# Gate logits computed with the gate's weights stationary on four column quarters, then turned by one transpose

## The chip, the cores and the metric

The kernel runs on one core of one Trainium2 chip. The core has a matrix engine (TensorE, "PE" in the profile, with its weight loads listed apart as "PEld"), a vector engine (VectorE, "DVE"), an engine for activation functions (ScalarE, "ACT"), a general engine (GpSimd, "POOL") and a queue engine that issues most transfers (SyncE, "SP"). Data lies in SBUF, 128 partitions wide; matrix products land in PSUM. The metric is the device time of one execution in microseconds (us). The kernel before took 2319.12 us (median of 3 runs, 2315.53 to 2322.49).

## What is computed

The input x has 16 sequences of 512 tokens with 256 features, all float32. One transformer layer is applied:

```python
x = x + attention(layernorm(x))          # 16 heads of 64, tanh soft clamp at 50, causal
t = layernorm(x)                         # 8192 tokens
shared = gelu(t @ sw1 + sb1) @ sw2 + sb2
probs = softmax(t @ gate_w + gate_b)     # gate_w is 256 x 8: one logit per expert
topk_p, topk_i = top_k(probs, 2)
combine = zeros(T, 8) with topk_p at topk_i
h = gelu(einsum('td,edf->etf', t, w1) + b1)
y = einsum('etf,efd->etd', h, w2) + b2
x = x + einsum('te,etd->td', combine, y) + shared
```

The change concerns `t @ gate_w` alone: for one sequence, 512 tokens by 256 features times 256 features by 8 experts.

## The kernel before, in words

The main loop runs over 16 sequences and, within each, over 8 pairs of heads (steps p = 0 to 7). A step does the score products of the next pair (`s`, line 272), attends for the present one (`av` and `sums`, lines 323 and 332), and projects queries and keys of the pair after next (`pq`, line 249). ACT clamps and exponentiates the scores (lines 287 and 288). VectorE divides by the row sums (`oT`: two reciprocals on line 342 and a product on line 343).

The rest of the layer is spread over the steps of the following sequence by the function `around`. Call the sequence whose attention is finished `done`. At p = 0 and 1 its output projection is made, at p = 1 its second layernorm; at p = 3 its normalised rows are turned (`x2T`, the tile of 128 features by 2 by 512 tokens), and after the two `pq` products of that step come the hidden layer of the shared expert (`hidden`, tile `ph`, line 695, then Gelu on ACT, line 703) and the gate (`gate`, tile `pg`, line 367). At p = 4 `place` ranks the tokens' choices within the group (`pos`, lines 414 and 415; `slot`, line 417), `transposed_comb` turns the table of shares (`pc`, line 685), two value projections follow (`pv`, line 232), and `expert_out` finishes the shared expert (`py`, lines 714 and 722).

The gate goes on after its product, all on VectorE but one activation: add the bias (`lg`, line 375), subtract the maximum (lines 377, 378), Exp on ACT (`pr`, line 380), normalise (lines 382 to 384), compare all pairs of experts to get each expert's rank (lines 389 to 394), and set the shares (`comb`, line 398).

Fifteen sequences are routed: their rows are scattered to DRAM by expert, and later read back in tiles of 256 rows for the routed experts (`rh`, `pr` of line 573, `ry`, on lines 586, 573 and 604). This work is a list of "fillers", of which `around` runs a few at the end of each step once a group of sequences (9, then 6) is complete. The last sequence is not routed but computed densely.

The order on PE is as written (the block runs under a manual schedule for PE); the other engines' orders are fixed by a scheduler when the program is built. Every engine executes its own list in order. PSUM tiles come from pools of two buffers: `ps_m` (tag "m": `pq`, `pg`, `pos`, `pc`, `pv`, `py` and others) and `ps_s` (tag "s": `s`, `ph`, the turned rows, `rh`). In this order the tile `ph` has the same bank as the second score tile `s` of the next step, so that this score product waits until Gelu has read `ph`.

A float32 product is two matrix instructions, each with its own weight load; a transpose is one. So the 8 products of one gate are 16 instructions in the profile. In those of line 367 the tokens are stationary (a 128 by 128 piece of `x2T`) and the gate's weights, 8 columns, stream past.

Of the kernel before, what the change touches and what calls it, by code (L numbers as in the profile page):

```python
# [9 lines left out]
F32 = mybir.dt.float32  # L10
# [5 lines left out]
P = 128  # L16
# [8 lines left out]
def preln_attention_moe_kernel(  # L25
# [15 lines left out]
    nc = tc.nc  # L41
# [4 lines left out]
    NT = N // P  # L46
    KD = D // P
    E = gate_w.shape[2]
# [4 lines left out]
    const = ctx.enter_context(tc.tile_pool(name="const", bufs=1))  # L53
    xp = ctx.enter_context(tc.tile_pool(name="xp", bufs=3))
    work = ctx.enter_context(tc.tile_pool(name="work", bufs=2))
    small = ctx.enter_context(tc.tile_pool(name="small", bufs=2))
# [3 lines left out]
    ps_m = ctx.enter_context(tc.tile_pool(name="ps_m", bufs=2, space=bass.MemoryType.PSUM))  # L60
# [11 lines left out]
    def sync_dma(to, of):  # L72
        with queued():
            last["dma"] = nc.sync.dma_start(to, of).ins
        return last["dma"]
# [32 lines left out]
    def weights(name, ap, queue):  # L108
        t = const.tile(list(ap.shape), F32, tag=name, name=name)
        queue.dma_start(t, ap)  # L110
        return t
# [3 lines left out]
    wq_sb = weights("wq_sb", wq, nc.sync)  # L115
    wk_sb = weights("wk_sb", wk, nc.scalar)
    wo_sb = weights("wo_sb", wo, nc.sync)
    gw_sb = weights("gw_sb", gate_w, nc.sync)
    gb_sb = const.tile([P, E], F32, tag="gb_sb", name="gb_sb")
    nc.sync.dma_start(gb_sb, gate_b.to_broadcast([P, E]))  # L120
    b1_sb = weights("b1_sb", b1, nc.sync)
# [4 lines left out]
    ident = const.tile([P, P], F32, tag="ident", name="ident")  # L126
# [59 lines left out]
    def layernorm(src, name):  # L186

        mv = small.tile([P, NT, 2], F32, tag="mv", name=f"mv_{name}")
        for t in range(NT):
            st = small.tile([P, 6], F32, tag="st", name=f"st_{name}_{t}")  # L190
            nc.vector.bn_stats(st, src[:, t, :])
            nc.vector.bn_aggr(mv[:, t, :], st)
        ve = small.tile([P, NT], F32, tag="ve", name=f"ve_{name}")
        nc.vector.tensor_scalar(ve, mv[:, :, 1], EPS, None, ALU.add)
        rstd = small.tile([P, NT], F32, tag="rstd", name=f"rstd_{name}")
        nc.gpsimd.tensor_tensor(rstd, ve, neg_half, ALU.pow)
        xn = work.tile([P, NT, D], F32, tag="xn", name=f"xn_{name}")
        for t in range(NT):
            nc.vector.tensor_scalar(  # L199
                xn[:, t, :],  # L200
                src[:, t, :],
                mv[:, t, 0:1],
                rstd[:, t : t + 1],
                ALU.subtract,
                ALU.mult,
            )
        return xn
# [138 lines left out]
    def project_out(b, h):  # L346

        xt = x_tiles[b]
        po = ps_m.tile([P, 2, D], F32, tag="m", name=f"po_{b}_{h}")
        for u in range(2):  # L350
            t = 2 * h + u
            for c in range(NP):
                nc.tensor.matmul(  # L353
                    po[:, u, :],
                    oTs[b, c][:, t * P : (t + 1) * P],
                    wo_sb[:, c, :],
                    start=(c == 0),
                    stop=(c == NP - 1),
                )
        nc.vector.tensor_add(xt[:, 2 * h : 2 * h + 2, :], xt[:, 2 * h : 2 * h + 2, :], po)  # L360

    def gate(b, xT):

        pg = ps_m.tile([P, NT, E], F32, tag="m", name=f"pg_{b}")
        for t in range(NT):
            for k in range(KD):
                nc.tensor.matmul(
                    pg[:, t, :],
                    xT[:, k, t * P : (t + 1) * P],
                    gw_sb[:, k, :],  # L370
                    start=(k == 0),
                    stop=(k == KD - 1),
                )
        lg = small.tile([P, NT, E], F32, tag="lg", name=f"lg_{b}")
        nc.vector.tensor_add(lg, pg, gb_sb.unsqueeze(1).to_broadcast([P, NT, E]))
        mx = small.tile([P, NT], F32, tag="mx", name=f"mx_{b}")
        nc.vector.tensor_reduce(mx, lg, AX.X, ALU.max)
        nc.vector.tensor_sub(lg, lg, mx.unsqueeze(2).to_broadcast([P, NT, E]))
        pr = small.tile([P, NT, E], F32, tag="pr", name=f"pr_{b}")
        nc.scalar.activation(pr, lg, AF.Exp)  # L380
        sm = small.tile([P, NT], F32, tag="sm", name=f"sm_{b}")
        nc.vector.tensor_reduce(sm, pr, AX.X, ALU.add)
        nc.vector.reciprocal(sm, sm)
        nc.vector.tensor_mul(pr, pr, sm.unsqueeze(2).to_broadcast([P, NT, E]))
        other = pr.unsqueeze(2).to_broadcast([P, NT, E, E])
        own = pr.unsqueeze(3).to_broadcast([P, NT, E, E])
        eq = small.tile([P, NT, E, E], F32, tag="table", name=f"eq_{b}", bufs=2)
        gt = small.tile([P, NT, E, E], F32, tag="table", name=f"gt_{b}", bufs=2)
        nc.vector.tensor_tensor(eq, other, own, ALU.is_equal)
        nc.vector.tensor_tensor(gt, other, own, ALU.is_gt)  # L390
        nc.vector.tensor_mul(eq, eq, before.unsqueeze(1).to_broadcast([P, NT, E, E]))
        nc.vector.tensor_add(gt, gt, eq)
        rank = small.tile([P, NT, E], F32, tag="rank", name=f"rank_{b}")
        nc.vector.tensor_reduce(rank, gt, AX.X, ALU.add)
        comb = small.tile([P, NT, 32], F32, tag="comb", name=f"comb_{b}")
        nc.gpsimd.memset(comb, 0.0)
        nc.gpsimd.memset(comb[:, :, E : E + 1], 1.0)
        nc.vector.scalar_tensor_tensor(
            comb[:, :, :E], rank, 1.5, pr, ALU.is_lt, ALU.mult
        )  # L400
        return comb, rank, pr
# [288 lines left out]
    def hidden(b, e, xT, w):  # L690
        ph = ps_s.tile([P, FC, N], F32, tag="s", name=f"ph_{b}_{e}")
        hT = work.tile([P, FC, N], F32, tag="hT", name=f"hT_{b}_{e}", bufs=2)
        for f in range(FC):
            for k in range(KD):
                nc.tensor.matmul(  # L695
                    ph[:, f, :],
                    w[:, k, f * P : (f + 1) * P],
                    xT[:, k, :],
                    start=(k == 0),
                    stop=(k == KD - 1),  # L700
                )
        for f in range(FC):
            nc.scalar.activation(hT[:, f, :], ph[:, f, :], AF.Gelu, bias=b1_sb[:, e, f : f + 1])
        return hT
# [49 lines left out]
        for _ in range(min(n, len(fillers))):  # L754
            fillers.popleft()()

    xTs, xns, gated, hTs = {}, {}, {}, {}
    units = range(len(UNITS))

    def early(b, p):  # L760
# [7 lines left out]
    def around(b, p, fill):  # L768

        done, more = b - 1, b + 1 < B  # L770
        group = group_of.get(done)
        if p == 0 and done >= 0:
            project_out(done, 0)
        if p == 1 and done >= 0:
            project_out(done, 1)
            xns[done, 1] = layernorm(x_tiles[done], f"f{done}")
        if p == 2:
            if more:
                xns[b + 1, 0] = layernorm(x_tiles[b + 1], f"a{b + 1}")
            if b < B:  # L780
                project_v(b, 2, xTs[b])
        if p == 3 and done >= 0:
            hTs[done] = hidden(done, SH, xTs[done, 1], sw1_sb)
            gated[done] = gate(done, xTs[done, 1])
        if p == 4:
            if done >= 0:
                comb, rank, pr = gated[done]
                if group:
                    place(done, rank, pr)
                gated[done] = comb, transposed_comb(done, comb)  # L790
            if b < B:
                project_v(b, 3, xTs[b])
        if p == 5 and more:
            project_v(b + 1, 0, xTs[b + 1])
        if p == 6 and more:
            project_v(b + 1, 1, xTs[b + 1])
        fill(p)
        if p == 4 and done >= 0:
            expert_out(done, SH, hTs.pop(done), sw2_sb, *gated[done])
            if group:  # L800
                scatter(done, xns.pop((done, 1)))
                sync_dma(
                    group.kept[done - group.first].rearrange("(t p) d -> p t d", p=P),
                    x_tiles.pop(done),
                )
                if done == group.first + group.count - 1:
                    tabulate(group)
                    fillers.extend(routed_steps(group))
                    fillers.append(lambda: pack(group))
                    fillers.extend(gather_steps(group))  # L810
                    pace["left"], pace["due"] = (B - 1 - b) * sum(WEIGHT), 0.0
                    if b == B - 1:
                        pace["left"] = 5 * len(fillers) // 6
        if p == 4 and b + 2 < B:
            load_x(b + 2)

    with tc.manual_schedule(engines={mybir.EngineType.PE}):
# [8 lines left out]
        for s in range(B * NP):  # L826
            b, p = divmod(s, NP)
# [12 lines left out]
        b = B - 1  # L840
# [68 lines left out]
```

## Time and profile before

| | |
|---|---|
| median of 3 runs | 2319.12 us |
| the profiled execution | 2317.56 us, of which the span of instructions is 2315.8 us |
| PE busy | 2209.4 us (95% of the span), 10968 matrix instructions |
| VectorE, ACT, POOL busy | 1102.8, 1037.9, 952.3 us |
| gate products, line 367 | 256 instructions, 29.6 us busy, 251 ns mean |
| hidden layer of the shared expert, line 695, one sequence | 8 instructions in 3.4 us |
| one sequence without fillers | 117.5 us (the gate starts at 190.65 and next at 308.19 us) |

Busy times count each instruction from its start to its modelled end, and matrix instructions overlap, so a difference of starts says more about what an instruction costs its queue. The chain of waits follows the work back from the last instruction to what released it; its durations add up to the span.

### The profile page before, as it was taken

How to read it: one execution, taken by the hardware profiler on the slowest of the kernel's cores; microseconds unless marked ns; L12 is line 12 of the kernel's file. 1: busy time of each engine (PE TensorE's matmuls, PEld its weight loads, DVE VectorE, ACT ScalarE, POOL GpSimd, SP SyncE). 2: the span in 40 equal slices, each digit the busy share in tenths (PEclk: the TensorE clock that was granted, in tenths of full speed). 3: DMA queues.
4: the chain of work that ended last, by engine and by line, in shares of the span. 5: the costliest groups of instructions: out<-in, count | busy, mean ns of one | idle time of the engine just before them, and what ended most of it. 6: DMA issues, size and time to landing. Idle time of an engine off the chain costs nothing.

```text
span 2315.8 us, 29554 instructions
## 1 busy us (share of the span) xinstructions
PE 2209.4 (95%) x10968; PEld 1405.6 (61%) x10968; DVE 1102.8 (48%) x1858; ACT 1037.9 (45%) x1352; POOL 952.3 (41%) x1091
## 2 busy tenths in 40 slices
PE   7999999999999999999999999999999799899996
PEld 3555555556565555555667677667655465558874
DVE  3445454545363636363644434444446555453334
ACT  3544444444444545444444554554554444351211
POOL 3444443435353535344423412422455847450025
PEclk9999999999999999999999999999999999999999
DMA  5001010101010101010142342342230503035776
GB/s 191 1 1 37 1 37 1 37 1 37 1 37 1 37 1 37 1 37 1 37 147 59 118 128 64 101 128 82 84 97 20 153 7 119 21 100 168 224 228 208
DMA packets 119855, 161.34 MB, mean 70 GB/s; under 512 B 12320, under 2 KB 90144, under 8 KB 119200
## 3 DMA queue, kind: packets, MB, share of 16 engines
q1 hardware_dynamic: 107760, 125.62, 17.5%
q0 software_dynamic: 11520, 31.47, 4.4%
q10 hardware_dynamic: 432, 2.36, 0.3%
q8 instruction: 87, 1.43, 0.3%
q14 instruction: 56, 0.46, 0.1%
HBM read 99.64 MB, written 59.77 MB: 69 GB/s over the span
## 4 chain that ended last, share of the span: by engine, by line
PE 76%; DVE 11%; DMA 5%; issue 3%; ACT 3%; POOL 2%; SPq 0%; POOLq 0%; DVEq 0%; ACTq 0%
PE pq L249 15%; PE s L272 10%; PE av L323 10%; PE po L353 9%; PE pv L232 8%; PE ry L604 5%; PE rh L586 5%; DVE oT L342 4%; PE sums L332 4%; DMA part<-ys,packed 3%; PE ph L695 2%; PE py L714 2%; DVE xn_a L199 2%; PE pr L573 1%; PE py L722 1%
## 5 line engine op out<-in xcount | busy, mean ns | idle before, releaser
L287 ACT ACTIVATE pe<-s 128x768 f32<-128x768 f32 (+1 forms) x384 | 334.5, 874 | 704.8 <-PE s L272 679.1
L342 DVE RECIPROCAL oT<-sums 128x256 f32<-128x256 f32 x256 | 430.9, 1724 | 355.3 <-PE sums L332 355.2
L291 POOL TENSOR_SCALAR_AFFINE_SELECT pe<-pe 128x256 f32<-128x256 f32 (+1 forms) x384 | 192.0, 501 | 902.0 <-ACT pe L288 847.4
L272 PE MATMUL s<-qk 64*128 64x512 f32 (+3 forms) x2048 | 345.4, 456 | 11.9 <-ACT qk L256 11.5
L288 ACT ACTIVATE pe<-pe 128x768 f32<-128x768 f32 (+1 forms) x384 | 349.5, 914 | 10.9
L323 PE MATMUL av<-pe,v 128*64 128x512 f32 (+3 forms) x2048 | 307.8, 443 | 34.5 <-DVE oT L343 34.4
L272 PEld LDWEIGHTS s<-qk 64*128 64x128 f32 x2048 | 176.6, 186 | 200.7 <-issue 144.9
L323 PEld LDWEIGHTS av<-pe,v 128*64 128x64 f32 x2048 | 140.3, 138 | 241.7 <-issue 208.7
L249 PE MATMUL pq<-xT_a,wq_sb 128*128 128x512 f32 x512 | 252.8, 617 | 0.8 <-DVE xT_a L217 0.8
L249 PE MATMUL pq<-xT_a,wk_sb 128*128 128x512 f32 x512 | 241.6, 595 | 5.0 <-DVE x L360 3.5
L232 PE MATMUL pv<-wv_sb,xT_a 128*128 128x256 f32 x1024 | 233.6, 382 | 4.4 <-DVE xT_a L217 4.4
L303 POOL TENSOR_TENSOR added<-pe,pe 128x768 f32<-128x768 f32 x128 | 232.3, 1814 | 10.5
L256 ACT COPY qk<-pq 128x512 f32<-128x512 f32 x256 | 149.8, 585 | 178.0 <-PE pq L249 178.0
L232 PEld LDWEIGHTS pv<-wv_sb,xT_a 128*128 128x128 f32 x1024 | 195.1, 192 | 52.0 <-issue 24.4
L353 PE MATMUL po<-wo_sb,oT 128*128 128x256 f32 x1024 | 226.3, 380 | 0.0
L353 PEld LDWEIGHTS po<-wo_sb,oT 128*128 128x128 f32 x1024 | 195.2, 191 | 38.7 <-issue 14.3
L653 POOL DMA_INDIRECT part<-ys,packed x120 | 117.2, 977 | 154.4 <-DMA dw<-in_w 99.6
L249 PEld LDWEIGHTS pq<-xT_a,wk_sb 128*128 128x128 f32 x512 | 97.7, 191 | 129.1 <-issue 120.4
L595 ACT ACTIVATE rhT<-rh,biases 128x256 f32<-128x256 f32 x148 | 62.0, 470 | 253.5 <-PE rh L586 253.4
L307 POOL TENSOR_TENSOR added<-added,pe 128x512 f32<-128x512 f32 x128 | 163.5, 1277 | 10.7
L239 DVE COPY v<-pv 128x512 f32<-128x512 f32 x128 | 87.3, 689 | 144.9 <-PE pv L232 144.9
L586 PE MATMUL rh<-rT,ew 128*128 128x256 f32 x592 | 142.6, 385 | 6.3 <-DVE rT L577 5.5
(134 smaller groups left out, 2302.4 us busy)
## 6 DMA issues: line engine op xcount, KB each, us to landing
ew<-in_w SPq DMA_DIRECT2D x148, 256.0 KB, 3.1
rows<-xs SPq DMA_DIRECT2D x74, 256.0 KB, 3.1
ys<-y SPq DMA_DIRECT2D x74, 256.0 KB, 3.3
x<-in_x SPq DMA_DIRECT2D x16, 512.0 KB, 4.0
xs<-zeros SPq DMA_DIRECT2D x32, 256.0 KB, 4.3
kept<-x SPq DMA_DIRECT2D x15, 512.0 KB, 3.0
acc<-kept SPq DMA_DIRECT2D x60, 128.0 KB, 2.9
out<-acc SPq DMA_DIRECT2D x60, 128.0 KB, 2.4
```

The costliest lines, as they stand in the source:

```text
L232: nc.tensor.matmul(pv[:, u], xT[:, k, t * P : (t + 1) * P], wv_pairs[:, k, :, 2 * g : 2 * g + 2, :], start=(k == 0), stop=(k == KD - 1),)
L249: nc.tensor.matmul(pq, w[:, k, p * P : (p + 1) * P], xT[:, k, :], start=(k == 0), stop=(k == KD - 1),)
L272: nc.tensor.matmul(ps[:, i, at : at + w], qk[rows, 1, j * P : (j + 1) * P], qk[rows, 0, j * P :], start=True, stop=True,)
L287: nc.scalar.activation(pe[:, :, :w], ps[:, :, :w], AF.Tanh, scale=CLAMP_IN)
L288: nc.scalar.activation(pe[:, :, :w], pe[:, :, :w], AF.Exp, scale=SOFTCLAMP)
L291: nc.gpsimd.affine_select(out=diagonal, in_=diagonal, compare_op=ALU.is_ge, fill=0.0, base=0, pattern=[[0, 2], [0, n], [1, P]], channel_mu ...
L303: nc.gpsimd.tensor_tensor(added, pair_pe[b, p, 0][:, :, P:], pe[:, :, : N - P], ALU.add)
L307: nc.gpsimd.tensor_tensor(added[:, :, P:], added[:, :, P:], pe[:, :, : 2 * P], ALU.add)
L323: nc.tensor.matmul(po[i * DH : (i + 1) * DH, j * P :], v[:, j, i, p % 2, :], pair_pe[b, p, u][:, i, at : at + w], start=(j == 0), stop=(j ...
L342: nc.vector.reciprocal(oT[:, half], sums[:, half])
L353: nc.tensor.matmul(po[:, u, :], oTs[b, c][:, t * P : (t + 1) * P], wo_sb[:, c, :], start=(c == 0), stop=(c == NP - 1),)
L586: nc.tensor.matmul(ph[:, f, :], tile["w1"][:, d, f * P : (f + 1) * P], tile["T"][:, d, :], start=(d == 0), stop=(d == KD - 1),)
```

## The change

The gate's weights become the stationary operand. They are padded with zeros from 8 to 32 columns, and the four token tiles of 128 tokens go to four column quarters of the PE array, each of which holds the same padded weights: the product of tile t writes partitions 32t to 32t + 31 of one PSUM tile `pl` (128 by 128: expert down, token across). There are still 8 products, 16 instructions. VectorE copies `pl` to SBUF (`logits`), and one transpose on PE brings tokens back to the partitions (`pg`, now 128 by 128, of which 4 by 8 columns are used).

The function is cut in two. `gate` (products and copy) is called before `hidden`, and `choose` (the transpose and all that came after the product) behind it. On PE the order was `pq`, `ph`, `pg`; it is now `pq`, `pl`, `ph`, `pg`. On VectorE the copy stands between the product of line 343 and `lg`; ACT's list is the same. At the start POOL clears the padded weights with its first fill of the kernel's own, and the load of `gate_w` on SP's queue, fourth there, writes 2 by 8 of the 2 by 32 columns.

```diff
-    gw_sb = weights("gw_sb", gate_w, nc.sync)
+    gw_sb = const.tile([P, KD, 32], F32, tag="gw_sb", name="gw_sb")
+    nc.gpsimd.memset(gw_sb, 0.0)
+    nc.sync.dma_start(gw_sb[:, :, :E], gate_w)
...
+    gated = {}
+
     def gate(b, xT):
-        pg = ps_m.tile([P, NT, E], F32, tag="m", name=f"pg_{b}")
-        for t in range(NT):
-            for k in range(KD):
+        pl = ps_m.tile([P, P], F32, tag="m", name=f"pl_{b}")
+        for k in range(KD):
+            for t in range(NT):
                 nc.tensor.matmul(
-                    pg[:, t, :],
+                    pl[t * 32 : (t + 1) * 32, :],
+                    gw_sb[:, k, :],
                     xT[:, k, t * P : (t + 1) * P],
-                    gw_sb[:, k, :],
                     start=(k == 0),
                     stop=(k == KD - 1),
                 )
+        logits = small.tile([P, P], F32, tag="combT", name=f"logits_{b}")
+        nc.vector.tensor_copy(logits, pl)
+        gated[b] = logits
+
+    def choose(b):
+        pt = ps_m.tile([P, P], F32, tag="m", name=f"pg_{b}")
+        nc.tensor.transpose(pt, gated[b], ident)
+        pg = pt.rearrange("p (t e) -> p t e", e=32)[:, :, :E]
         lg = small.tile([P, NT, E], F32, tag="lg", name=f"lg_{b}")
         nc.vector.tensor_add(lg, pg, gb_sb.unsqueeze(1).to_broadcast([P, NT, E]))
...
         if p == 3 and done >= 0:
+            gate(done, xTs[done, 1])
             hTs[done] = hidden(done, SH, xTs[done, 1], sw1_sb)
-            gated[done] = gate(done, xTs[done, 1])
+            gated[done] = choose(done)
```

## The prediction

> **What bounds the kernel now.** I read the page first. PE is busy for 95% of the span, which suggests that every matrix instruction saved is time saved. Part 4 of the page says otherwise in part:
>
> ```profile
> PE 2209.4 (95%) x10968; PEld 1405.6 (61%) x10968; DVE 1102.8 (48%) x1858; ACT 1037.9 (45%) x1352; POOL 952.3 (41%) x1091
> ...
> PE 76%; DVE 11%; DMA 5%; issue 3%; ACT 3%; POOL 2%; SPq 0%; POOLq 0%; DVEq 0%; ACTq 0%
> ```
>
> PE is 76% of the chain that ended last; 11% is VectorE, 3% ACT. So there are places where PE, though busy, is ahead of what decides. I then asked the chain of waits in order of time for one sequence around its gate (start, length, what):
>
> ```profile
> 181.20 0.86 PE sums L332 x8
> 182.06 0.85 PE s L272 x8
> ...
> 183.94 3.44 PE pq L249 x8
> 187.37 3.45 PE ph L695 x8
> ...
> 190.85 1.26 ACT hT L703 x2
> ...
> 193.42 0.24 ACT pr L380
> ...
> 202.29 0.16 DVE slot L417
> 202.45 0.04 issue
> 202.50 0.33 PE pc L685
> ...
> 213.16 2.31 PE av L323 x16
> ...
> 230.82 3.63 PE pq L249 x8
> ```
>
> The reader is to see what is missing. After `ph` the chain leaves PE: Gelu on ACT, a table load (192.13 to 193.41), Exp for `pr`, then twenty VectorE instructions up to `slot`, and it comes back to PE at `pc`. `pg` isn't in it. In the timeline `lg` and its two followers end at 193.17, and Exp starts at 193.42, just after the table load: the gate's product is 0.24 us early. From 193.68 to `slot` VectorE has no gap over 0.04 us (its two long reciprocals, 3.28 us, stand in that queue behind the ranking). PE does its work meanwhile and then waits, which the groups by line confirm:
>
> ```profile
> L367 PE MATMUL pg<-gw_sb,x2T_f 128*128 128x8 f32 x256 | 29.6, 251 | 0.0
> L685 PE MATMUL pc<-ident,comb 128*128 128x128 f32 x16 | 5.2, 325 | 4.5 <-DVE slot L417 4.5
> ```
>
> `pc` waits for `slot` 0.28 us in nearly every sequence. So between the end of `ph` and `pc` the path runs over ACT and VectorE, and PE has nothing to give there. Where fillers follow the gate it is different; the chain there, for the tenth gate:
>
> ```profile
> 1288.07 3.43 PE ph L695 x8
> 1291.51 1.69 PE pg L367 x16
> 1293.19 1.83 PE rh L586 x8
> ```
>
> Here `pg` is on the chain. By the timeline, of the 16 gates 12 are followed at once by scores `s` (the first nine and numbers 13 to 15), and 4 by fillers (10 to 12, and the last).
>
> **The change, part by part.**
>
> *What leaves `pg`'s place.* 16 instructions at a pitch of 0.111 us: 1.70 us before `rh`, 1.78 before `s` (differences of starts). One transpose comes there instead: `pr` of line 573 takes 0.44 us for 4 in the chain, so 0.11 us.
>
> *What is put before `ph`.* I call the delay of `ph` d. It has three terms.
>
> 1. Streaming. Instructions on column halves overlap: `sums` streams 4 x 128 + 4 x 384 = 2048 columns in 0.86 us, 0.42 ns a column, and `pq` on the full array 4096 in 3.44, 0.84 ns. Two halves go in the time of one. No row shows four quarters. The new products stream 16 x 128 = 2048 columns: 0.43 us if four overlap, 0.86 if two, 1.72 if none. I take four, since two halves lost nothing, and keep the others as ends. For four instructions starting one after another I add 0.03.
>
> 2. Going into another division of the array. `av` comes after row halves: 5120 columns at 0.42 ns are 2.15 us, the chain shows 2.31, so 0.16. I take that; a quarter's weight load is shorter, so 0.10 is the low end, the 0.20 of the next term the high one.
>
> 3. Going back to the full array. `pq` takes 3.63 us after row halves (230.82) and 3.44 after transposes on the full array (183.94): 0.19 to 0.20. `s` after column halves agrees: 4 x 256 + 4 x 128 columns at 0.42 are 0.65, the row shows 0.85.
>
> So d = 0.43 + 0.03 + 0.16 + 0.20 = 0.82 us, from 0.73 to 1.3, or 2.1 without overlap. Before, PE went from `pq` to `ph` in one division and paid neither 2 nor 3; the switch on the way to `s` is paid with and without the change.
>
> The Trainium skill (TensorEngine Tiling, Key Properties) says that a change of tiling mode drains the array. The rows of terms 2 and 3 agree, at 0.16 to 0.20 us. The page (When to Use Tiling) also recommends just this swap for an operand of at most 32 columns, with up to four times the speed; by that alone the 1.70 us would fall to an estimate of 0.43, plus 0.11 for the transpose, and 16 gates would save 19 us. The drain, and the place, speak against that.
>
> *Twelve gates followed by scores.* `ph` ends d later; Gelu, table load, `pr`, the VectorE queue, `slot` and `pc` all follow d later, since each starts when the one ahead ends. The product's 0.24 us of earliness grows, which buys nothing. PE gains 1.78 - 0.11 - 0.82 = 0.85 us and loses it again twice: the second score tile waits until Gelu has read `ph` in the same bank (Gelu ended at 192.11, the tile started at 193.38; now Gelu ends at 192.93 and PE would be there at 192.53, so 0.4 us of new wait), and at `pc` PE waits the rest, some 1.2 us in place of 0.28. Behind `pc` PE goes on without a gap. Each costs +0.82: 12 x 0.82 = +9.8 us.
>
> *Four gates followed by fillers.* PE is the path: 0.82 + 0.11 - 1.69 = -0.76 each, -3.0 us. ACT would hold them if its Gelu for `rh` came too late: it moves from 1296.50 to 1297.32, and PE asks for that bank at about 1297.32. That is even, so at most 0.1 us is lost. In the tail the chain goes by transfers that start from these products, so its 0.76 may get lost too: between -3.0 and -2.2.
>
> *The rest, at nothing.* The copy of `pl` (0.28 us by the 128x128 copy of line 687) is one more VectorE instruction between 186.6 and 192.5, where that engine is idle for 5.9 us; the transpose needs it only after 3.4 us of `ph`. Without that cover it would cost 0.28 + 0.1 per gate. `pl` needs what `ph` needed (`x2T`, ready 186.77, asked at 187.2) and the bank of the first `pq` tile (copied by 186.28). At the start one POOL fill (0.15 us) precedes the identity, which is done at 1.6 us and needed at 14.28; SP's load of `gate_w` is issued at 2.31, long after that fill; behind it in SP's queue are biases and zero fills, and the next x, whose transfer is issued at 26.5 us and read at 33.5. Its extra descriptors lie between nothing and the 0.74 us that this issue takes now. One `v` copy stands behind a fourth normalisation there (0.35 us); its reader comes later than 43 us.
>
> *Sum.* +9.8 - 3.0 = +6.8 us on the profiled execution's own time: 2317.56 + 6.8 = 2324.4. That execution is 1.56 us under the median of the three, so I predict 2325.9, +0.29%. A measurement here tells about 0.3%, 7 us, from no change; the forecast stands just at that bound.
>
> **The rivals.**
>
> *A. PE decides everywhere (faster).* Then each gate is worth -0.76 to -0.85 and 16 give -13 us: 2306. For it speaks the 95%. Against it, `pg` is not in the chain of 12 gates and `pc` waits for `slot`. It would need `slot` to come over 0.85 us before PE; it comes 0.28 after.
>
> *B. Quarters overlap less (slower, more).* Two at a time: d = 1.25, 12 x 1.25 - 4 x 0.33 = +13.7, 2332.8. None: d = 2.11, +27.4, 2346.5. For it: no row shows four. Against: halves overlap without loss.
>
> *C. The delay is absorbed.* The same sequence has a wait of 1.3 us of `av` for `oT` at p = 3. If its releaser didn't move with PE, the 9.8 us would vanish and -3.0 remain: 2316. Against: that chain starts from a score product of PE itself, and runs over ACT, POOL and the layernorm back to PE, so it moves too.
>
> *D. Switching is cheap between full and quarters:* d = 0.46, 12 x 0.46 - 4 x 1.12 = +1.0, 2320. Against: three kinds of switch in the rows cost 0.16 to 0.20.
>
> **How the numbers follow.** Forecast, with d from 0.73 to 0.95 (+4.9 to +8.8 us with the tail's doubt, 2324 to 2328): 0.62, of which 0.33 over the bound and 0.29 under it. A: 0.05. B: 0.19 (two at a time 0.15, none 0.04). C and D: 0.14. Slower by over 0.3%: 0.33 + 0.19 = 0.52; within: 0.29 + 0.14 = 0.43; faster: 0.05. The range reaches down to D, 2320, and up to two at a time, 2333; it leaves out A, none, and C's lower half, some 0.15.
>
> **What would show it.** Line 367's successor: 16 instructions per gate on 32 columns in about 0.43 us, `ph` starting 0.6 to 0.7 us after `pq`'s stream ends and its second product 0.1 later still. `lg` far earlier than the end of the table load. The second score tile waiting for Gelu, 0.4 us, 12 times; `pc` waiting 1.2 us; `pl` in the chain ahead of `ph`. Distance of gates without fillers: 117.5 + 0.8 = 118.4 us. The forecast is wrong if that distance falls, which means A, or if `pl` spreads over 0.9 us, which means B.

## The result and the profile after

The changed kernel takes 2328.15 us (median of 6, 2325.55 to 2329.58) beside 2318.97 us before: ratio 1.004, 95% interval 1.0026 to 1.0054. A second set, taken later, gave 2326.97 beside 2319.08 us: 1.0035, 1.0023 to 1.0047. So the change makes the kernel slower by 8 to 9 us; predicted were 2325.9 us and a range of 2320 to 2333. The profiled execution took 2325.55 us (span 2323.8), 8.0 us more than that of before.

First the page of the changed kernel, part 1 and the chain by engine:

```profile
PE 2204.0 (95%) x10984; PEld 1378.7 (59%) x10984; DVE 1101.4 (47%) x1874; ACT 1036.3 (45%) x1352; POOL 950.1 (41%) x1092
...
PE 74%; DVE 12%; issue 5%; DMA 3%; ACT 3%; POOL 3%; SPq 0%; DVEq 0%; another core or an unknown queue 0%; POOLq 0%; ACTq 0%
```

PE has less to do than before (2204.0 against 2209.4 us) and a smaller part in the chain (74% against 76%): it waits more. The groups of the gate's products, its transpose, and the product that waits for the ranking (count and form, then busy us and mean ns, then idle time ahead):

```profile
L371 PE MATMUL pl<-x2T_f,gw_sb 128*32 128x128 f32 x256 | 10.3, 279 | 0.0
L698 PE MATMUL pc<-ident,comb 128*128 128x128 f32 x16 | 5.2, 325 | 9.3 <-DVE slot L430 9.3
L385 PE MATMUL pg<-ident,logits 128*128 128x128 f32 x16 | 4.4, 272 | 0.0
```

The gate's products fell from 29.6 to 10.3 us busy. The wait at `pc` doubled, from 4.5 to 9.3 us in all. The chain of waits around the first gate (start, length, what) says what stands ahead of that wait:

```profile
184.22 3.44 PE pq L251 x8
187.66 0.57 PE pl L371 x16
188.24 3.64 PE ph L708 x8
...
191.90 1.19 ACT hT L716 x2
...
193.18 1.28 ACT L393
...
198.50 3.28 DVE oT L344 x2
201.78 0.56 DVE ahead L424
...
203.35 0.10 DVE slot L430
...
203.50 0.33 PE pc L698
```

`pl` is now a link of the chain, between `pq` and `ph`. From Gelu (`hT`) to `slot` the chain takes 203.35 - 191.90 = 11.45 us; before it took 202.29 - 190.85 = 11.44. The path over ACT and VectorE kept its length and starts later.

PE's timeline for the same gate shows what PE gained and where it gave it back (start, time to the last end, instruction, tile, count; idle time ahead and its releaser in brackets). Before:

```profile
185.49 1.88 PE L249 MATMUL pq<-xT_a,wk_sb 128*128 128x512 f32 x4
...
192.42 1.77 PE L272 MATMUL s<-qk 64*128 64x512 f32 x8
...
201.69 0.30 PE L414 MATMUL pos<-chosen,earlier 128*128 128x32 f32 x2
...
202.50 0.33 PE L685 MATMUL pc<-ident,comb 128*128 128x128 f32 x1 [0.28 <-DVE slot L417]
```

and after the change:

```profile
185.78 1.88 PE L251 MATMUL pq<-xT_a,wk_sb 128*128 128x512 f32 x4
187.59 0.65 PE L371 MATMUL pl<-x2T_f,gw_sb 128*32 128x128 f32 x16
188.16 3.70 PE L708 MATMUL ph<-x2T_f,sw_sb 128*128 128x512 f32 x8
191.70 0.27 PE L385 MATMUL pg<-ident,logits 128*128 128x128 f32 x1
191.90 1.13 PE L274 MATMUL s<-qk 64*128 64x512 f32 x4
193.22 0.92 PE L274 MATMUL s<-qk 64*128 64x384 f32 x4 [0.19 <-ACT hT L716]
...
201.62 0.30 PE L427 MATMUL pos<-chosen,earlier 128*128 128x32 f32 x2
202.39 0.41 PE L428 MATMUL pos<-ahead,ones 128*128 128x32 f32 x2 [0.46 <-DVE ahead L424]
203.50 0.33 PE L698 MATMUL pc<-ident,comb 128*128 128x128 f32 x1 [0.69 <-DVE slot L430]
```

I read such a timeline by differences of starts, since ends are modelled. From the start of the last `pq` tile to the first `s`: 6.93 us before, 6.12 after, a gain of 0.81. From there to `pos`: 9.27 and 9.72, so 0.45 lost while the second score tile waits for Gelu. From `pos` to `pc`: 0.81 and 1.88, so 1.07 lost while PE waits for VectorE. Together +0.71 us. The first eight such gates all show it (I call the 12 that scores follow direct gates, the others filler gates): their distance is 117.54 or 117.55 us before and 118.26 or 118.27 after.

The rest of the run, by starts of `ph` of the k-th gate in the traces, with three traces of each kernel (the second and third are among the runs below) and what the prediction's steps give for each stretch:

| stretch | before, three traces | after, three traces | forecast |
|---|---|---|---|
| start to 1st | 187.21, 187.74, 188.00 | 188.16, 188.56, 188.50 | +0.82 |
| 1st to 9th | 940.33, 940.38, 940.38 | 946.11, 946.13, 946.09 | +6.56 |
| 9th to 10th | 160.36, 160.37, 160.37 | 158.90, 159.22, 158.98 | +0.82 |
| 10th to 12th | 340.01, 340.01, 340.01 | 338.71, 338.72, 338.71 | -1.52 |
| 12th to 13th | 145.94, 148.53, 148.78 | 146.69, 146.72, 146.85 | -0.76 |
| 13th to 14th | 131.15, 131.72, 131.49 | 135.73, 131.34, 135.51 | +0.82 |
| 14th to 16th | 280.30, 279.85, 281.27 | 278.91, 279.36, 278.72 | +1.64 |
| 16th to the end | 130.50, 129.41, 129.79 | 130.63, 126.99, 132.88 | -1.58 |
| span | 2315.81, 2318.01, 2320.08 | 2323.84, 2317.04, 2326.25 | +6.8 |

The upper half is steady to some tenths; the lower half, where rows are gathered and scattered, moves by several us from one execution to the next, in both kernels.

### The profile page after: what moved, and what is told of

Read it like the earlier page. It is cut to its first block, busy times and chain, and to the rows that moved or that the text cites. A ratio compares the mean times of both kernels' runs of the same rounds, so it can differ in the third digit from the quotient of the medians.

```text
span 2323.8 us, 29607 instructions
## 1 busy us (share of the span) xinstructions
PE 2204.0 (95%) x10984; PEld 1378.7 (59%) x10984; DVE 1101.4 (47%) x1874; ACT 1036.3 (45%) x1352; POOL 950.1 (41%) x1092
## 4 chain that ended last, share of the span: by engine, by line
PE 74%; DVE 12%; issue 5%; DMA 3%; ACT 3%; POOL 3%; SPq 0%; DVEq 0%; another core or an unknown queue 0%; POOLq 0%; ACTq 0%
PE pq L251 15%; PE s L274 10%; PE av L325 9%; PE po L355 9%; PE pv L234 7%; PE ry L617 5%; PE rh L599 5%; DVE oT L344 4%; PE sums L334 4%; PE ph L708 3%; DVE xn_a L201 2%; PE py L727 2%; DMA part<-ys,packed 1%; PE pr L586 1%; PE py L735 1%
## 5 line engine op out<-in xcount | busy, mean ns | idle before, releaser
L274 PE MATMUL s<-qk 64*128 64x512 f32 (+3 forms) x2048 | 350.9, 459 | 22.6 <-ACT qk L258 19.8
```

Of the source, the lines that this page charges most:

```text
L274: nc.tensor.matmul(ps[:, i, at : at + w], qk[rows, 1, j * P : (j + 1) * P], qk[rows, 0, j * P :], start=True, stop=True,)
```

## Experiments

The theory: on this path it counts where PE's time stands. A microsecond ahead of `ph` delays Gelu, the ranking and `pc` by a microsecond; one behind `ph` is hidden behind the ranking. The first rival: the new form costs by itself (going into the quarters and back, transpose, copy), wherever it stands. The second: PE's total counts.

**1. The new gate behind the hidden layer.**

```diff
-            gate(done, xTs[done, 1])
             hTs[done] = hidden(done, SH, xTs[done, 1], sw1_sb)
+            gate(done, xTs[done, 1])
             gated[done] = choose(done)
```

> The new gate, in all its parts, called behind the hidden layer instead of ahead of it. Theory (the place costs: whatever stands ahead of the hidden layer delays Gelu, Exp, VectorE's ranking and with them the turned shares): the hidden layer ends when it did in the kernel before, the twelve gates followed by scores cost nothing and gain at most the 0.05 us by which that path was ahead of PE, and the four followed by fillers gain 1.70 - (0.16 + 0.43 + 0.20 for division and streaming, 0.4 for the wait on the copy, 0.11 for the transpose) = 0.4 us each. Sum -2 us against the kernel before, ratio 0.999 (0.998 to 1.0005). Rival (the form costs: two changes of the array's division and the round trip over the copy are lost wherever they stand): +0.4 to +0.8 us for each of 16, ratio 1.003 to 1.005.

Measured: 2321.09 beside 2319.90 us, ratio 1.0006 (0.9996 to 1.0016). The loss is gone from the total with the place, the form unchanged. But it wasn't a gain either: the distance of direct gates is 117.80 us, +0.27 where -0.05 was expected, so of the 0.72 us per gate 0.46 are gone. Two lines of PE's timeline, then three of the chain:

```profile
191.13 0.30 PE L385 MATMUL pg<-ident,logits 128*128 128x128 f32 x1 [0.50 <-DVE logits L379]
...
201.99 0.33 PE L698 MATMUL pc<-ident,comb 128*128 128x128 f32 x1 [0.84 <-DVE slot L430]
```

```profile
190.09 1.26 ACT hT L716 x2
...
200.17 0.86 DVE ahead L424
...
201.99 0.33 PE pc L698
```

PE stands still for the copy of the logits, which nothing covers here, but neither that copy nor the transpose is in this chain: `pc` waits for the ranking. What grew is the path: from Gelu to `pc` it takes 201.99 - 190.09 = 11.90 us, where the kernel before takes 11.65 and the changed one 11.60. Part of it is one `ahead` add on VectorE that takes 0.94 us; it runs beside a GpSimd add, which is told below.

**2. The products twice, all ahead, and 3. twice, half of them behind.** Both repeat all products of the gate; the second pass overwrites the same values (2) or a tile already copied (3), so the output stays.

In 2, within the gate (`products` holds its eight products, 16 instructions):

```diff
         products(pl, xT)
+        products(pl, xT)
         logits = small.tile([P, P], F32, tag="combT", name=f"logits_{b}")
```

In 3, behind the hidden layer:

```diff
-            gate(done, xTs[done, 1])
+            pl = gate(done, xTs[done, 1])
             hTs[done] = hidden(done, SH, xTs[done, 1], sw1_sb)
+            products(pl, xTs[done, 1])
             gated[done] = choose(done)
```

> The changed kernel, with the sixteen quarter products done twice ahead of the hidden layer (the second time over the first). Theory (place): the hidden layer is 0.43 us later, each of 16 gates costs 0.43 us more, +7 us against the changed kernel, so ratio to the kernel before 1.007 (1.0055 to 1.0085). Rival (PE time counts wherever it stands): the same, +7 us. Rival (something ahead has slack for it): 1.004.

> The changed kernel, with the quarter products done a second time behind the hidden layer, ahead of the transpose, into the PSUM tile that has been copied. It adds 0.77 us of PE time (streaming and two changes of division) to each gate, more than the variant with both ahead. Theory (place): the twelve gates followed by scores take it at nothing, out of the waits of 0.19, 0.46 and 0.70 us that PE has behind them; the four followed by fillers pay 0.77: +3 us against the changed kernel, ratio to the kernel before 1.005 (1.004 to 1.0065). Rival (PE time counts wherever it stands): +12 us, ratio 1.009.

Measured: 2331.83 us, 1.0058 (1.0045 to 1.0071), and 2326.74 us, 1.0033 (1.002 to 1.0046). In the traces the distance of direct gates is 118.70 us with both ahead, +0.43 on the changed kernel, just what a second pass streams. With the second pass behind it is 118.27, +0.00, though PE works 0.73 us longer there. That extra work is paid at the gates followed by fillers (170.16 against 169.36 us between the 10th and the 11th), as it should be where PE decides. The total of the second run lies below what was expected (1.004 to 1.0065): 3 us at the fillers and the tail don't show in it, since the lower half moves by as much from one execution to the next. The distances are free of that. These two settle the main point: the same instructions cost 0.43 us in one place and nothing in the other.

**4. Gelu by halves**, to make ACT's path shorter: each half of `ph` goes to Gelu as soon as it is done.

```diff
+            if e == SH:
+                nc.scalar.activation(
+                    hT[:, f, :], ph[:, f, :], AF.Gelu, bias=b1_sb[:, e, f : f + 1]
+                )
-        for f in range(FC):
+        for f in range(FC if e != SH else 0):
```

> The changed kernel, with Gelu of the shared expert issued on each half of the hidden layer as soon as that half is done, so that it ends about 0.6 us earlier while PE's work is the same. Theory (the path goes hidden layer, Gelu, table load, Exp, ranking, turned shares): the delay of 0.77 falls to 0.17 us for twelve gates, +1.4 us in place of +8.7, and the four others keep their gain of 0.65: ratio to the kernel before 0.9995 (0.998 to 1.0015). The wait of the second score tile for Gelu disappears. Rival (the loss sits in PE's own queue, in the changes of division): nothing changes, 1.004.

Measured: 2361.52 us, 1.0192 (1.0178 to 1.0206). A miss, by two things that I hadn't thought of. The waits of PE around the first gate (us in all, times, longest):

```profile
PE pc L698 <- DVE slot L430: 2.9, 1, 2.9
...
PE ph L708 <- ACT hT L716: 0.8, 1, 0.8
```

The second half of `ph` now waits for Gelu of the first (probably because both halves are one tile to the program; no run separates them): the saving was spent at once. And the scheduler, with other times before it, put all `ahead` adds ahead of the reciprocals on VectorE, where one met GpSimd. GpSimd's timeline, then the chain:

```profile
198.88 1.82 POOL L305 TENSOR_TENSOR added<-pe,pe 128x768 f32<-128x768 f32 x1
```

```profile
198.84 0.18 DVE ahead L424
...
199.05 1.68 DVE ahead L424
...
200.75 0.56 DVE ahead L422
```

Two equal adds of 128x8: 0.18 us, and 1.68 us beside `added`. In addition PE's clock was halved for 3.4 us after every second of these waits (from 206.7, 449.1, 691.4 us on), so the distances alternate between 122.08 and 120.39 us.

**5. The ranking inside the hidden layer.** The gate stays ahead; the transpose and the whole choice are issued after the first of the hidden layer's products.

```diff
-    def hidden(b, e, xT, w):
+    def hidden(b, e, xT, w, between=None):
...
+                if between and f == 0 and k == 0:
+                    between()
...
-            hTs[done] = hidden(done, SH, xTs[done, 1], sw1_sb)
-            gated[done] = choose(done)
+            def between():
+                gated[done] = choose(done)
+
+            hTs[done] = hidden(done, SH, xTs[done, 1], sw1_sb, between)
```

> The kernel of the change with its matmuls where they are, ahead of the hidden layer, but with the transpose and the whole ranking issued after the hidden layer's first product instead of behind its last. The Exp of the choice and its table load then stand ahead of the Gelu on ScalarE, and the ranking on VectorE runs beside products. Place theory (a microsecond of TensorE ahead of the hidden layer counts, and behind it the ranking decides): the direct gates lose the ranking from the path, TensorE's 0.77 us and 0.11 us of transpose stand for 1.78 us before, and the second score tile waits some 0.57 us for the Gelu: about -0.38 us for each of 12, -4.6 us; the three filler gates -0.65 us each and the tail's about -1: -7.6 us in all, ratio 0.9965 (0.995 to 0.9985). Rival (the four quarters cost by themselves, wherever the rest stands): 1.003 to 1.004 as the change had it.

Measured: 2310.76 beside 2320.21 us, ratio 0.9963 (0.995 to 0.9977): faster than both kernels. The chain of waits around the first gate:

```profile
187.04 0.57 PE pl L371 x16
187.61 1.06 PE ph L708 x2
188.67 0.11 PE pg L385
188.78 2.59 PE ph L708 x6
...
191.39 1.27 ACT hT L718 x2
...
192.71 0.92 PE s L274 x4
...
201.42 0.24 PE pos L428 x2
...
201.68 0.20 DVE slot L430
...
201.93 0.33 PE pc L698
```

The ranking is gone from it. Between Gelu and `pc` all is PE's, but for the one instruction `slot`, which itself waits for `pos`: a round trip, in which PE waits the same 0.28 us as before. The direct gates are at 117.32 us, -0.22 and not -0.38. The terms of the expectation give -1.78 + 0.77 + 0.11 + 0.57 = -0.33. Measured are -0.80 from `pq` to `s`, where they have -0.90, and +0.57 from `s` to `pos`, as they have it: the 1.78 us of the old products before `s` hold a change of division (they take 1.70 before `rh`) that stays. The 10th to the 12th take 338.20, -0.90 each and not -0.65.

**6. The gate of before and its whole choice ahead of the hidden layer.** `gate` is cut in two here as well, products and choice, but both stand ahead.

```diff
+            gate(done, xTs[done, 1])
+            gated[done] = choose(done)
             hTs[done] = hidden(done, SH, xTs[done, 1], sw1_sb)
-            gated[done] = gate(done, xTs[done, 1])
```

> The gate of the kernel before, its sixteen full-array matmuls with no quarters and no transpose, and its whole ranking, moved ahead of the hidden layer. Place theory: the hidden layer starts 1.78 us later, the ranking is off the path, and the second score tile waits for the Gelu that ends later: +0.5 us for each of the 12 direct gates, nothing for the others: +6 us, ratio 1.0026 (1.001 to 1.004). Rival (only TensorE's sum counts, which stays, and the ranking's path is gone): 0.999 to 1.000.

Measured: 2327.86 us, 1.0032 (1.002 to 1.0044). Distance of direct gates 118.22 us, +0.67:

```profile
187.84 1.85 PE L369 MATMUL pg<-gw_sb,x2T_f 128*128 128x8 f32 x16
...
194.58 0.92 PE L272 MATMUL s<-qk 64*128 64x384 f32 x4 [0.30 <-ACT hT L710]
...
203.80 0.33 PE L692 MATMUL pc<-ident,comb 128*128 128x128 f32 x1 [0.28 <-DVE slot L424]
```

The rival "only PE's sum counts" falls: PE has the same instructions as before, in another order, and loses 7.7 us by the medians. Beside run 5, which has the same waits, it gives the form's own worth: 118.22 - 117.32 = 0.90 us per gate in favour of the quarters.

The runs so far, by PE's starts around the first gate, in the three portions used above (us):

| kernel | `pq` to `s` | `s` to `pos` | `pos` to `pc` | sum |
|---|---|---|---|---|
| before | 6.93 | 9.26 | 0.81 | 17.00 |
| after | 6.12 | 9.72 | 1.88 | 17.72 |
| gate behind | 6.62 | 9.27 | 1.36 | 17.25 |
| twice, ahead | 6.56 | 9.72 | 1.87 | 18.15 |
| twice, half behind | 6.85 | 9.26 | 1.61 | 17.72 |
| Gelu by halves | 7.17 | 9.26 | 3.40 | 19.83 |
| ranking inside | 6.13 | 9.83 | 0.81 | 16.77 |
| old gate ahead | 7.03 | 9.83 | 0.81 | 17.67 |

The first column is PE's work, the second has the wait for Gelu over 9.26, the third the wait for VectorE over 0.81.

**7. The change for the first nine gates only** (the gate of before for the other seven).

```diff
-            gate(done, xTs[done, 1])
+            new = done < 9
+            if new:
+                gate(done, xTs[done, 1])
             hTs[done] = hidden(done, SH, xTs[done, 1], sw1_sb)
-            gated[done] = choose(done)
+            gated[done] = choose(done) if new else old_gate(done, xTs[done, 1])
```

> The change for the first nine sequences, the gate of before for the other seven. If the time of the change sits in the gates that score tiles follow: 9 x 0.72 us and 0.18 us at the start, less up to 2 us that the pause at the first group's tabulation takes up: +4.7 to +6.7 us, ratio 1.0025 (1.0015 to 1.0035). If it sits behind the gathers instead, where the trace of the change shows +3.9 us more between the 13th and the 14th gate: 0.9995 to 1.001.

Measured: 2324.28 us, 1.0018 (1.0009 to 1.0027), +4.1 us by the medians. From the 1st to the 9th gate it takes 946.14 us, like the changed kernel, and 13th to 14th take 131.12. So about half of the loss is from the first nine gates. The other half comes later, though the filler gates, which gain, lie there too.

**8. Where the rest comes from: five repeats of kernels already run.** In the table of the result one row stands out: 135.7 us between the 13th and the 14th gate, where before has 131.2.

> The kernel before, profiled a second time. If the +3.9 us between the 13th and the 14th gate (1774 to 1905 us) belong to the change, this trace repeats the distance of 131.15 us of the first within some 0.3 us; if that stretch, which follows the gathers, varies by itself, it is 2 to 5 us off.

> The changed kernel, profiled a second time. Its first trace has 135.73 us between the 13th and the 14th gate, where the kernel before has 131.15; the traces with the gate behind the hidden layer and with doubled matmuls have 135.7 to 136.6 there, the three kernels of the second set 130.9 to 131.1. If those 4 us belong to the kernel, this trace has 135.7 again; if they belong to the execution or the chip, it may have 131, and the changed kernel's span is then about 2319 us.

> The kernel before, on the same chip right after it. If the 4 us belong to the chip, this trace has about 136 us between the 13th and the 14th gate wherever the changed kernel's has; if to the kernel, 131.2 to 131.7 us as in its two traces so far.

> The kernel with the gate's new form behind the hidden layer, a second time. It had 135.88 us there. If the 4 us belong to the kernel: 135.9 us again; otherwise 131, which would make it about 4 us faster than its first trace.

> The changed kernel once more, unaltered, timed on its own against the kernel before. Its second trace repeats the +0.72 us at every gate that a score tile follows and the gain at the filler gates, +3.8 us in all up to the 12th gate, but has 131.3 us between the 13th and the 14th gate where the first trace had 135.7, and a tail of 127.0 us where the first had 130.6. If the 4 us of that stretch come and go with the execution or the chip, the gates alone are left: ratio 1.0016 (1.0005 to 1.0028). If they belong to the changed kernel in most of its executions: 1.003 to 1.005, as when it was first timed.

Measured (13th to 14th): before 131.72 and 131.49, after 131.34 and 135.51, gate behind 131.42 where it had been 135.88. So the 4 us come and go between executions of the same kernel. They aren't shared evenly: of the changed kernel's 12 timed executions none took less than 2324.37 us, and the two of them that were traced (2325.55 and 2328.00) both have the 4 us, while the single execution without them took 2318.74. (Between that one and the first lie 6.8 us: 4.4 in the row of the stall, 3.6 in the tail, -1.2 in the others. On its chip the kernel before took 2321.79 and 2322.32 us in one execution each, so there the changed kernel was not slower.) The traces of runs 2, 3 and 4 have them as well (135.7 to 136.6). None of three traces of before has them, nor those of runs 5, 6 and 7. It is likely, though only those traces show it, that most executions of the changed kernel carry them.

What it is: ACT's waits there (1815 to 1835 us), in the first trace of the changed kernel, which has them, and then in the second, which doesn't:

```profile
ACT pe L289 <- remote: 8.5, 1, 8.5
```

```profile
ACT pe L289 <- PE s L274: 9.0, 3, 4.0
```

and PE's timeline in the same two:

```profile
1832.05 3.30 PE L234 MATMUL pv<-wv_sb,xT_a 128*128 128x256 f32 x7 [6.19 <-ACT qk L258]
```

```profile
1826.47 3.62 PE L234 MATMUL pv<-wv_sb,xT_a 128*128 128x256 f32 x16
```

The clamp of a score tile (line 289) waits 8.5 us, though PE's records have that tile's products starting by 1822. In the second trace no single wait is longer than 4.0. ACT's queue then holds back the copy of `qk`, and `pv` on PE comes 6 us late. Part of that is won back before the next gate. The profile names no releaser ("remote"). Whether the products themselves ended late (their ends are modelled) or the news of them reached ACT late, and why mostly in the changed kernel, these runs don't tell; it stays open.

## Why the prediction was right, and where it was not

*What bounds the kernel.* Right. Between `ph` and `pc` the path goes over Gelu, the table load and the ranking; it kept its length (11.44 and 11.45 us) and started later. One argument was weak though the conclusion held: `pc` waits 0.28 us for `slot` also in run 5, where PE decides. That is the round trip from `pos` over VectorE and back (0.81 us from `pos` to `pc` in before and in runs 5 and 6), not proof that VectorE is late. The trace of before has the same 0.28 at its 10th and 11th gate, where PE is the path. The room was close to nothing, which is why a gate costs 0.72 and not quite the delay of `ph`.

*d, the delay of `ph`.* Forecast 0.82 us, measured 0.09 (the `pq` tile ahead ends its stretch later) + 0.57 + 0.10 (`ph`'s own first loads) = 0.76. Four quarters overlap in full, as taken: the trace starts four instructions 6 to 7 ns apart and the next four 0.11 to 0.13 us later, so 16 take 0.45 us, against 0.43 + 0.03. The two changes of division together cost about 0.3 instead of 0.36. The Trainium skill (TensorE: Matmul & The Clock Gate, "Measured speedup vs the span model") counts the time of one product plus some 4 ns for each further tile of the array; the trace agrees but for the 6 to 7 ns. Rival B (two at a time) is out, D (cheap switches) too.

*Gates followed by scores.* Forecast +0.82 each, measured +0.72. Its two losses: wait for Gelu 0.4 forecast, 0.46 measured; at `pc` 0.92 more forecast (1.2 for 0.28), 1.07 measured, spread over `pos` and `pc`, which I hadn't split. The 1.2 was a slip: a path 0.82 later and a PE that arrives 0.85 - 0.4 = 0.45 sooner make 0.28 + 0.82 + 0.45 = 1.55. PE's own gain 0.85 forecast, 0.81 measured; with d at 0.76 it should have been 0.91, but the transpose takes 0.20 us of PE up to the first `s` (191.70 to 191.90) and not 0.11. Neither changes what a gate costs, since the ranking decides that.

*Filler gates.* -0.76 forecast, -0.65 measured (340.01 to 338.71 for two). (The low end of the forecast's inner band, too, is off: d = 0.73 gives 12 x 0.73 - 4 x 0.85 = +5.4, not +4.9.)

*Two steps that failed, in opposite directions.* The first is that distances outside the gates stay. From the 9th to the 10th +0.82 was forecast and -1.2 to -1.5 came. There PE waits near 1170 us, while VectorE tabulates the group, and then runs `pv`. PE's timeline there, and its table by stretches (length, busy time and instructions of each engine, and then, third from the end, the granted clock), for before:

```profile
1164.99 5.50 PE L232 MATMUL pv<-wv_sb,xT_a 128*128 128x256 f32 x16 [2.89 <-DVE xT_a L217]
```

```profile
1165.70:1169.10 3.40, 3.40 (x9) 2.69 (x10) 0.69 (x1) 0.25 (x1) 0.00 (x0) 0.50 0.89 261
```

and after:

```profile
1171.27 3.81 PE L234 MATMUL pv<-wv_sb,xT_a 128*128 128x256 f32 x16 [2.60 <-DVE xT_a L219]
```

```profile
1171.30:1175.00 3.70, 3.70 (x16) 2.82 (x16) 1.11 (x2) 0.93 (x2) 0.00 (x0) 1.00 0.86 258
```

Before, the granted clock is 0.50 for 3.4 us after the wait and `pv` takes 5.50 us; after, it is 1.00 and `pv` takes 3.81. That is 1.7 us won by the clock, in all three traces of each, and no part of my sum. But it isn't the change's doing. Run 7 is the changed kernel up to this wait and has the half clock behind it, after the same 2.90 us that the changed kernel waits in its second trace without it:

```profile
1171.57 5.50 PE L234 MATMUL pv<-wv_sb,xT_a 128*128 128x256 f32 x16 [2.90 <-DVE xT_a L219]
```

What decides is told in the last section. The second failed step is the stretch behind the gathers (13th to 14th), where the stall of run 8 added 4 us in the two traces that belong to the timed sets.

So the gates alone explain less than the total says: up to the 12th gate the changed kernel stands at +4.0 us (0.95 + 5.78 - 1.46 - 1.30, first traces) where the steps gave +6.7; the stall (+4.6 in its row) and -0.5 in the three other rows bring it to 8.0. The direction and the mechanism were right and the size of each gate was off by 0.1 us. That the total came out so near the forecast is luck: the clock took off 1.7 us and the stall added over 4, neither was in the sum, and the one execution without the stall (2318.74 us) lies below the forecast range. The direct gates behind the 12th, and the tail, can't be read from the distances, since those rows vary by more than a gate is worth; the wait at `pc` is 0.69 us at the 13th and 14th as at the first eight.

*Rivals.* A (PE decides everywhere, faster) is refuted by runs 2 and 3. C (the delay is absorbed) didn't happen in any of the eight distances between direct gates. What I called the tail's doubt remains: 126.99 to 132.88 us in three traces of the same kernel.

## What to carry to other kernels

Before moving work on a busy engine, mark on the chain of waits where that engine hands over to others: work put ahead of the handover is paid in full, even if it is cheaper than what it replaces, and work behind it may be free. Here a form worth 0.9 us per gate made the gate 0.7 us slower where it was put, and 0.2 faster than before once the work that waited for it (transpose and ranking) was moved ahead of the handover too. And a wait of a few tenths at the end of a path may be a round trip; compare it with a place where the engine is known to decide before calling it slack.

## What the runs showed of the hardware

*A small VectorE add can wait for GpSimd's whole instruction.* `ahead` (128x8, two operands in SBUF) takes 0.18 us when it starts ahead of GpSimd's `added` of 1.82 us and 1.68 beside it, and ends just when that ends (200.73 and 200.70); the copy that follows takes 0.56. The reciprocals, which read PSUM, keep their length beside the same instructions (3.28 us for two). The Trainium skill (SBUF — State Buffer, "SBUF: two separate sides") says that a VectorE instruction with two SBUF inputs and a GpSimd instruction that reads SBUF lock each other out for the whole instruction; the add agrees with it. So the order that a scheduler gives tiny instructions can cost more than the change under study, as run 4 shows.

*PE's clock halves in pieces of 3.4 us after waits shorter than that, and where the wait falls decides.* In these traces the granted clock falls to 0.50 for 3.4, 6.8 or 10.2 us at a time, and within each of the 14 traces all these changes lie on one grid of 3.413 us, to within 2 ns; where the grid lies differs from execution to execution. The wait before it was 2.89 us in before and 2.67 in run 1, while 2.60 in the changed kernel and 2.90 in run 5 had no such effect; in run 4 the same wait of 2.9 us had it every second time. Cut where the grid cuts them, they sort themselves:

| PE's wait | us | its parts on the grid | half clock behind it |
|---|---|---|---|
| before, to 1164.99 | 2.89 | 0.19 + 2.70 | yes |
| run 1, to 1166.19 | 2.67 | 0.56 + 2.11 | yes |
| run 7, to 1171.57 | 2.90 | 0.80 + 2.09 | yes |
| run 3, to 1171.32 | 2.58 | 0.63 + 1.95 | yes |
| run 6, to 1745.69 | 3.80 | 1.90 + 1.91 | no |
| run 5, to 1162.64 | 2.90 | 1.83 + 1.07 | no |
| changed kernel, to 1171.27 | 2.60 | 0.89 + 1.71 | no |
| changed kernel, second trace, to 1172.01 | 2.90 | 1.23 + 1.67 | no |
| run 4, to 205.45 and to 327.52 | 2.87 | 0.74 + 2.14, 1.55 + 1.32 | yes, no |

The 14 traces have 162 waits of PE over 1.2 us between 60 and 1760 us. All 23 with at least 1.95 us in one piece of the grid are followed by half clock, none of the 139 with at most 1.91 is (ends are modelled, so the bound is rough). The Trainium skill (TensorE: Matmul & The Clock Gate, "HAM oscillation — how this bites in real kernels") advises to keep PE's idle gaps under about 3.4 us; here that wasn't short enough, and a wait of 3.80 us did no harm. The clock also goes with much of the scatter: between the 12th and the 13th gate the first trace of before (145.94 us) has no half clock near 1740 us, the others (148.53, 148.78) have 6.8 us of it, and the three of the changed kernel (146.69 to 146.85) 3.4.
